# Layer 3's delta rule in half tiles, its query sums on TensorE, and two norms beside the collecting

## The chip, the cores and the metric

The kernel runs on one core of a Trainium2 chip, in one launch. A core has a matrix engine (PE, TensorE; its weight loads are listed apart as PEld), a vector engine (DVE), an activation engine (ACT, ScalarE), a general engine (POOL, GpSimd) and a queue engine (SP) that issues transfers. Each engine runs its own instructions in the order in which they were built into its stream, and waits on semaphores for the others. SBUF is the large on-chip memory. PSUM holds what PE writes; a tile of 128 x 512 fp32 fills one of its eight banks, and ACT and DVE can read and write it.

The metric is the device time of a launch in microseconds (us), the median over the runs. Before the change it is 4753.9 us, from three runs of 4752.63, 4753.9 and 4770.15. Lower is better.

## The reference

Four layers work on 4096 token columns of 128 features, held on the chip as `x`, 128 partitions by 4096 (8 tiles of 512). Each layer normalises and adds two branches:

```python
xn = _layernorm(x, axis=-1)          # (x - mean) / sqrt(var + 1e-5)
x = x + attention(xn, ...) + feed_forward(xn, ...)
```

Layers 0 and 2 end with experts: every token collects its two weighted rows from a result table in device memory and adds them to `x`. Layer 0 adds a shared dense branch besides.

Layer 3's attention is a delta rule. Queries and keys are convolved, passed through Silu and divided by their norms; per head (8 wide) a state `S` of 8 x 8 is carried over the tokens:

```python
def step(S, inp):
    q_t, k_t, v_t, b_t = inp
    v_new = (v_t - jnp.einsum('bhd,bhdm->bhm', k_t, S)) * b_t[..., None]
    S = S + jnp.einsum('bhd,bhm->bhdm', k_t, v_new)
    o_t = jnp.einsum('bhd,bhdm->bhm', q_t, S)
    return (S, o_t)
```

Layer 3's feed-forward is a pair of dense products with a sine between them:

```python
hidden = jnp.einsum('bsd,df->bsf', x, W1) + b1
imag = w_imag * jnp.sin(theta + hidden * 0.1)
quantum_phase = jnp.cos(theta) * w_real + jnp.sin(theta) * w_imag
act = jax.nn.relu(hidden + quantum_phase * imag * 0.1)
return jnp.einsum('bsf,fd->bsd', act, W2) + b2
```

## The kernel before

**Norm.** `_layer_norm` goes over the eight tiles. A matmul with a matrix of 1/128 (L292) gives the mean in PSUM, DVE subtracts it (L293), ACT squares (L295), four narrow matmuls (L297) give the variances of 512 tokens. When all tiles are through, one copy (L304), one Sqrt (L305) and one reciprocal (L306) follow for all 4096 tokens, and a second pass spreads the reciprocals over the features (POOL copy L273, PE transposes L276) and multiplies (L316).

**Collecting.** `_collect` fetches, for each group of 128 tokens and each of their two experts, 128 rows with one indirect transfer that POOL issues (L1031). DVE weights and adds them (L1039, L1041), PE transposes (L1042, into `cl_tp`, two PSUM banks), DVE adds to `x` (L1044). `_together` runs generators side by side, one tile of each in turn: in layer 0 the shared dense branch and the collecting, in layer 2 the collecting alone.

**Layer 3.** `_layer3` loads and prepares the weights, calls the norm, and then builds everything in a fixed order (`manual_schedule`: each engine's stream follows the order of the Python statements). Three convolutions of four taps per tile (L1743 matmuls, L1751 Silu) write to device memory, and the results are fetched back in another layout (heads on partitions, 32 chunks of 32 tokens along the row).

`_delta_rule` then works in three stages, on rows of 1024 (chunk, value, key) fp32 per partition, two PSUM banks for a state tile:

1. *States*, 32 steps: for all chunks but the last at once, two recurrences run. `sm` carries the map of a chunk's start state to its end, `sn` the state that grows from zero. Each step: `pro` = state times key (DVE, L1879), `dd` = its sum over the key (DVE, L1882), minus the value for `sn` (L1885), `u` = `dd` times key (DVE, L1890); PE rewrites the state as an identity times its copy minus an identity times `u` (`add`, L1871, four matmuls), and ACT copies the new state (`hist`, `dprod`, L1896). Within these steps the queries' squares are summed by DVE, eight pieces (L1916).
2. *Scan*, 31 steps: each chunk's start state from the one before it (L1944, L1951, L1952), on DVE, into an SBUF tile. Ahead of it stand a Sqrt of the query sums (L1804), a maximum, a reciprocal and a product (L1805, L1806, L1938).
3. *Outputs*, 32 steps over all 32 chunks from their true start states, with one state tile `sm` of 32 chunks. POOL multiplies the copied state by the query (L1985), after a small copy (`pace`, L1983) that makes it wait for `u`; DVE sums that product two steps later (L1961).

`_waves` is the feed-forward, a pipeline of 32 items (8 tiles by 4 quarters of the hidden width). Every call moves five items on by one stage each: `close` (L2050, DVE, every fourth item), `leave` (L2046, PE), `rest` (L2039 DVE, L2040 ACT relu), `fold` (L2033 and L2034 on DVE, L2035 Sin on ACT) and `enter` (L2025 PE, then L2027, L2029, L2030 on ACT). `_delta_rule` yields after every step of states and scan and once in an output step, and the loop in `_layer3` calls the waves at some of these yields:

```python
for n, _ in enumerate(_delta_rule(k, s, wl)):
    if n % 2 if n < 32 or n >= 63 else n % 6 == 2:
        next(waves, None)
```

So in states and outputs one item passes every second step, in the scan one every sixth.

Of the kernel before, what the change touches and what calls it, by code (L numbers as in the profile page):

```python
# [10 lines left out]
F32 = mybir.dt.float32  # L11
# [268 lines left out]
def _layer_norm(k, second=None):  # L280
# [4 lines left out]
    with tc.tile_pool(name="ln", bufs=3) as w, tc.tile_pool(  # L285
        name="ln_ps", bufs=5, space=PSUM
    ) as k.misc, tc.tile_pool(name="ln_st", bufs=1, space=PSUM) as sp:
        st = sp.tile([P, W], F32, name="ln_st")
        for t in range(NT):
            c = slice(t * W, (t + 1) * W)  # L290
            mean = k.misc.tile([P, W], F32, name="misc")
            nc.tensor.matmul(mean, k.mean, k.x[:, c], start=True, stop=True)  # L292
            nc.vector.tensor_tensor(k.xn[:, c], k.x[:, c], mean, ALU.subtract)  # L293
            sq = w.tile([P, W], F32, name="sq")
            nc.scalar.activation(sq, k.xn[:, c], AF.Square)  # L295
            for i in range(4):
                nc.tensor.matmul(  # L297
                    st[:, 4 * t + i : 4 * t + i + 1],
                    sq[:, i * P : (i + 1) * P],
                    k.mean[:, 0:1],  # L300
                    start=True,
                    stop=True,
                )
        nc.vector.tensor_copy(k.var, st[:, :TT])  # L304
# [714 lines left out]
def _collect(k, got, res, acc):  # L1019
# [3 lines left out]
    with tc.tile_pool(name="cl", bufs=6) as g, tc.tile_pool(name="cl_ps", bufs=2, space=PSUM) as ps:  # L1023
# [59 lines left out]
def _layer0(k, a):  # L1083
    _layer_norm(k)
    with k.tc.tile_pool(name="keep0", bufs=1) as keep:
# [7 lines left out]
        _together(_shared(k, a, k.x), _collect(k, got, k.res[0], k.x))  # L1093
# [417 lines left out]
def _layer1(k, a):  # L1511
    _layer_norm(k, (k.eps6, k.vec("l1_g"), k.vec("l1_b"), k.xl))
    _attention1(k, a)
    _local_layers(k, a)
# [171 lines left out]
def _layer2(k, a):  # L1686
    _layer_norm(k)
    with k.tc.tile_pool(name="keep2", bufs=1) as keep:
# [14 lines left out]
        _together(_collect(k, got, k.res[1], k.x))  # L1703
# [65 lines left out]
def _delta_rule(k, s, wl):  # L1769
# [97 lines left out]
    def add(st, w, u, first, last):  # L1867

        c = u.shape[1]
        for n in (slice(0, 16), slice(16, c)):  # L1870
            nc.tensor.matmul(st[:, n], w, u[:, n], start=first, stop=last)  # L1871

    def differ(st, now, i, c, values, parts=1):


        pro = room("pro")
        for n in range(parts):
            own = slice(n * c // parts, (n + 1) * c // parts)
            nc.vector.tensor_tensor(pro[:, own], st[:, own], _bc(kp[:, i, own], 2, 4), ALU.mult)  # L1879
        add(st, k.ident, now()[:, :c], True, False)  # L1880
        d = w.tile([P, CH, 4], F32, name="dd")
        nc.vector.tensor_reduce(d[:, :c], pro[:, :c], AX.X, ALU.add)  # L1882
        yield
        if values:
            nc.vector.tensor_tensor(d[:, :c], d[:, :c], vp[:, i, :c], ALU.subtract)  # L1885
        yield update(st, d, i, c)

    def update(st, d, i, c, first=False):
        u = room("u")
        nc.vector.tensor_tensor(u[:, :c], _bc(d[:, :c], 3, 8), _bc(kp[:, i, :c], 2, 4), ALU.mult)  # L1890
        add(st, k.neg_ident, u[:, :c], first, True)
        return u

    def copy(name, st, c):
        now = room(name)
        nc.scalar.copy(flat(now[:, :c]), flat(st[:, :c]))  # L1896
        return now
# [6 lines left out]
    ends = CH - 1  # L1904
    add(sm, k.ident, _bc(k.unit.rearrange("p (v d) -> p v d", d=8), 1, ends), True, True)
    mm, nn = copy("hist", sm, ends), None
    squares = ip.tile([P, 4, 8, P], F32, name="dvo")

    def query_norms(c):
        if 0 <= c < 8:  # L1910
            own = slice(c * P, (c + 1) * P)
            nc.scalar.activation(squares[:, c % 4], qraw[:, :, own], AF.Square)
        if 1 <= c < 9:
            own = slice((c - 1) * P, c * P)
            sq = squares[:, (c - 1) % 4]
            nc.vector.tensor_reduce(rq[:, own], sq.rearrange("p d t -> p t d"), AX.X, ALU.add)  # L1916
# [305 lines left out]
```

## Time and profile before

| | us |
|---|---|
| median of the runs | 4753.9 |
| the profiled execution, whole | 4760.1 |
| its span | 4758.3 |
| layer 0: shared branch with collecting | 1148 to 1311 |
| norm behind it, first half | 1311 to 1324.6 |
| layer 2: collecting | 3870 to 3969.6 |
| norm ahead of layer 3 | 3969.6 to 3995.9 |
| convolutions and fetching | 3995.9 to 4094 |
| states | 4094 to 4381 |
| before the scan | 4381 to 4395.6 |
| scan | 4395.6 to 4449.5 |
| outputs | 4449.5 to 4706.9 |
| output norm and product | 4706.9 to 4758.3 |

Times inside the profile are counted from the start of its span. A table of stages gives, for each stretch, the busy time of every engine with the number of its instructions, the TensorE clock that was granted (1.00 is full speed) and the share of time in which the transfer engines were at work. A line of a timeline gives start, duration, engine, line and operation, the tile written and the tiles read, shapes, and in brackets how long the engine had been idle and what it waited for.

### The profile page before, as it was taken

To read this page: it belongs to the slowest core of one execution; us is meant where nothing else is said; L and a number is where in the kernel's file an instruction comes from. 1 tells how busy PE (TensorE), PEld (TensorE's weight loads), DVE (VectorE), ACT (ScalarE), POOL (GpSimd) and SP (SyncE) were. 2 spreads that over 40 slices of the span, in tenths; PEclk is the share of its full clock that TensorE was granted. 3 is DMA by queue.
4 is the path that set the end of the run, shared out by engine and by line. 5 is a ranking of instruction groups with operands and counts; after the bars stand their busy time and mean duration, and the time that the engine had idled before them with its cause. 6 is when DMAs were issued, how large, how long until landed. Compare 5 with 4: busy or idle time off the path is not lost. (4 is left out here: it accounts for less than half of the span.)

```text
span 4758.3 us, 54361 instructions
## 1 busy us (share of the span) xinstructions
PE 3887.6 (82%) x20924; PEld 1774.2 (37%) x20924; DVE 3111.6 (65%) x4404; ACT 2562.6 (54%) x3611; POOL 649.7 (14%) x639
## 2 busy tenths in 40 slices
PE   4679999998968888888877888888879966888564
PEld 3223333364332222222224555555534543333221
DVE  5868989722336656565657888888465323899876
ACT  1257877831259999999984555455422112344331
POOL 1310000003100000000003232233103122000132
PEclk6689999999967777777778999999889987999788
DMA  2411121021221010100002111111100223300001
GB/s 86 118 41 55 29 59 26 11 72 49 14 83 58 18 49 18 36 27 18 18 13 65 36 41 35 40 34 32 37 0 23 63 64 83 97 0 9 0 0 53
DMA packets 107494, 191.81 MB, mean 40 GB/s; under 512 B 23138, under 2 KB 48354, under 8 KB 105378
## 3 DMA queue, kind: packets, MB, share of 16 engines
q1 hardware_dynamic: 98756, 166.31, 12.3%
q0 software_dynamic: 8192, 16.79, 1.7%
q10 hardware_dynamic: 288, 5.24, 0.3%
q8 instruction: 165, 2.70, 0.2%
q14 instruction: 93, 0.76, 0.1%
HBM read 95.00 MB, written 67.39 MB: 34 GB/s over the span
## 5 line engine op out<-in xcount | busy, mean ns | idle before, releaser
L740 DVE TENSOR_TENSOR p<-p,e 128x1024 f32<-128x1024 f32 x512 | 586.7, 1221 | 321.7 <-ACT e L738 321.7
L723 PE MATMUL big<-q,k 32*128 32x512 f32 x2048 | 560.3, 633 | 180.6 <-ACT p L734 74.9
L533 DVE TENSOR_REDUCE m<-mx 128x2 f32<-128x1024 f32 x512 | 620.9, 1223 | 101.4 <-PE mx L525 94.2
L418 PE MATMUL av<-p,v 128*32 128x256 f32 (+1 forms) x5632 | 666.4, 528 | 0.3
L616 ACT ACTIVATE p<-s 128x512 f32<-128x512 f32 x1024 | 550.9, 597 | 184.7 <-PE s L607 171.5
L723 PEld LDWEIGHTS big<-q,k 32*128 32x128 f32 x2048 | 210.8, 229 | 707.0 <-ACT e L738 347.3
L607 PE MATMUL s<-q,k 64*128 64x512 f32 x1024 | 277.7, 494 | 48.4 <-DMA q<-mrows 33.4
L738 ACT ACTIVATE e<-big,neg_mu 128x1024 f32<-128x1024 f32 x256 | 262.0, 1125 | 11.7 <-PE big L723 11.4
L525 PE MATMUL mx<-k,q 64*128 64x512 f32 x1024 | 238.8, 437 | 32.3 <-DVE m L533 17.8
L734 ACT ACTIVATE p<-big,neg_mu 128x1024 f32<-128x1024 f32 x256 | 261.2, 1199 | 3.0 <-PE big L723 2.8
L738 ACT ACTIVATE e<-big 128x1024 f32<-128x1024 f32 x256 | 243.0, 1040 | 28.8 <-PE big L723 27.2
L734 ACT ACTIVATE p<-big 128x1024 f32<-128x1024 f32 x256 | 239.4, 1076 | 8.2 <-PE big L723 8.1
L1177 POOL TENSOR_TENSOR lqk<-lt 128x512 f32<-128x512 f32 x128 | 162.5, 1269 | 518.1 <-DVE lt L1168 461.3
L1150 PE MATMUL lps<-f_wqkv,lh 128*128 128x512 f32 x384 | 215.2, 649 | 11.7 <-DVE lo L1305 6.8
L1871 PE MATMUL sm<-hist,in_const_sb 128*128 128x512 f32 x252 | 144.0, 701 | 93.1 <-ACT hist L1896 79.5
L1031 POOL DMA_INDIRECT cl_row<-res,back x128 | 121.2, 947 | 713.7 <-DMA in_l_su_sb<-in_l_su 474.3
L418 PEld LDWEIGHTS av<-p,v 128*32 128x32 f32 x5632 | 121.3, 111 | 253.1 <-issue 202.6
L607 PEld LDWEIGHTS s<-q,k 64*128 64x128 f32 x1024 | 107.5, 184 | 284.9 <-issue 162.3
L1268 ACT ACTIVATE lsm<-lsm 128x512 f32<-128x512 f32 x128 | 80.6, 630 | 222.1 <-DVE lsm L1267 220.7
L1896 ACT COPY hist<-sm 128x992 f32<-128x992 f32 (+1 forms) x65 | 64.9, 999 | 224.0 <-DVE pro L1879 143.4
L950 POOL DMA_INDIRECT buf<-xtok,to x128 | 125.9, 983 | 407.7 <-DMA buf<-xtok,to 221.3
L1143 POOL MEMSET lva<- 128x32 f32 x16 | 2.4, 152 | 1148.1 <-PE av L418 1148.1
(412 smaller groups left out, 6888.5 us busy)
## 6 DMA issues: line engine op xcount, KB each, us to landing
hl<-phi SPq DMA_DIRECT2D x64, 256.0 KB, 2.9
hl<-plo SPq DMA_DIRECT2D x64, 256.0 KB, 3.5
lvs<-lva SPq DMA_DIRECT2D x16, 520.0 KB, 5.7
q<-hl SPq DMA_DIRECT2D x32, 256.0 KB, 5.2
k<-hl SPq DMA_DIRECT2D x32, 256.0 KB, 5.9
q<-hl SPq DMA_DIRECT2D x16, 512.0 KB, 5.3
k<-hl SPq DMA_DIRECT2D x16, 512.0 KB, 3.5
lvs<-lva SPq DMA_DIRECT2D x16, 390.0 KB
```

What stands on the lines that cost most here:

```text
L418: k.nc.tensor.matmul(av[32 * j : 32 * j + 32, cols], v[:, kc, 9 * (4 * g + j) : 9 * (4 * g + j) + 32], pts[j][:, cols], start=kc == 0, sto ...
L525: nc.tensor.matmul(ps[:, i, :], q[rows, gg, qt * P : (qt + 1) * P], key[rows, gg, half * W : (half + 1) * W], start=True, stop=True, tile_ ...
L533: nc.vector.tensor_reduce(m[:, qt, gg, :, half], ps, AX.X, ALU.max)
L607: nc.tensor.matmul(ps, key[rows, half, kc * P : (kc + 1) * P], q[rows, half, qh * W : (qh + 1) * W], start=True, stop=True, tile_position= ...
L616: nc.scalar.activation(p, ps, AF.Exp, scale=8.0**-0.5)
L723: nc.tensor.matmul(ps[:, jj, :], key[rows, kc * P : (kc + 1) * P], q[rows, qh * W : (qh + 1) * W], start=True, stop=True, tile_position=(3 ...
L734: nc.scalar.activation(p, ps, f, bias=bias, scale=scale)
L738: nc.scalar.activation(e, ps, f, bias=bias, scale=scale)
L740: nc.vector.tensor_tensor(p, p, e, ALU.mult)
L1150: nc.tensor.matmul(ps, z.h[:, t * P : (t + 1) * P], wqkv[:, own], start=True, stop=True)
L1177: nc.gpsimd.tensor_tensor(z.qk[t][:, own], r[0], r[1], ALU.add)
L1871: nc.tensor.matmul(st[:, n], w, u[:, n], start=first, stop=last)
```

## The change

*Norms.* A generator `_norm_beside` runs beside the collecting. At layer 0 (`whole` is false) it takes means, differences, squares and variances of each tile as soon as `x` has it, with one PSUM bank for itself and one fewer for `cl_tp`; `_layer_norm` then begins at the Sqrt. At layer 2 it does the whole norm tile by tile, and `_layer3` has none.

*Weights.* Layer 3's loads and the preparation of its weights move into `_weights3`, ahead of layer 2.

*States.* `dd` lies in a PSUM bank of its own, in four turns. The query sums become eight matmuls with the identity that add up in a bank of the waves (`qh`), and an ACT copy. The waves' banks go from three to two. The Sqrt stands in step 18.

*Scan.* The start states are written straight into the PSUM state tiles.

*Outputs.* Chunks 0 to 15 and 16 to 31 are two PSUM tiles (`sm`, `sn`), each two banks, and each half runs through `differ` by itself: product, copy, adds, sum, difference, `u`. The `pace` copy is gone. There are two yields per step.

*Waves.* The argument is kept in turns instead of radians. A call now does half of the stages, either (`close`, `leave`, `sine`) or (`rest`, `enter`, `fold`), with `fold` a subtraction on POOL and the clamp on DVE in `sine`. The halves come at every second yield in states and outputs and at two of three in the scan.

```diff
+def _centre(k, t, misc, w):
+    nc = k.nc
+    c = slice(t * W, (t + 1) * W)
+    mean = misc.tile([P, W], F32, name="misc")
+    nc.tensor.matmul(mean, k.mean, k.x[:, c], start=True, stop=True)
+    nc.vector.tensor_tensor(k.xn[:, c], k.x[:, c], mean, ALU.subtract)
+    sq = w.tile([P, W], F32, name="sq")
+    nc.scalar.activation(sq, k.xn[:, c], AF.Square)
+    return sq
...
+def _norm_beside(k, whole):
+    nc, tc = k.nc, k.tc
+    with tc.tile_pool(name="nb", bufs=3) as w, tc.tile_pool(
+        name="nb_ps", bufs=2 if whole else 1, space=PSUM
+    ) as misc:
+        squares = {}
+        def variance(t):
+            st = misc.tile([P, W], F32, name="misc")
+            sq, own = squares.pop(t), slice(4 * t, 4 * t + 4)
+            for i in range(4):
+                nc.tensor.matmul(
+                    st[:, i : i + 1], sq[:, i * P : (i + 1) * P], k.mean[:, 0:1], start=True, stop=True
+                )
+            nc.vector.tensor_copy(k.var[:, own], st[:, :4])
+            if whole:
+                nc.scalar.activation(k.inv[:, own], k.var[:, own], AF.Sqrt, bias=k.eps5)
+                nc.vector.reciprocal(k.inv[:, own], k.inv[:, own])
+        def scale(t):
+            c = slice(t * W, (t + 1) * W)
+            spread = w.tile([P, 4, P], F32, name="nb_s")
+            nc.scalar.copy(spread, _bc(k.inv[:, 4 * t : 4 * t + 4], 2, P))
+            ps = misc.tile([P, W], F32, name="misc")
+            for i in range(4):
+                nc.tensor.transpose(ps[:, i * P : (i + 1) * P], spread[:, i], k.ident)
+            nc.vector.tensor_tensor(k.xn[:, c], k.xn[:, c], ps, ALU.mult)
+        for t in range(NT + 2):
+            if whole and t >= 2:
+                scale(t - 2)
+            if 1 <= t <= NT:
+                variance(t - 1)
+            if t < NT:
+                squares[t] = _centre(k, t, misc, w)
+            if t < NT:
+                yield
...
-        _together(_shared(k, a, k.x), _collect(k, got, k.res[0], k.x))
+        _together(_shared(k, a, k.x), _collect(k, got, k.res[0], k.x, 1), _norm_beside(k, False))
...
-    _layer_norm(k, (k.eps6, k.vec("l1_g"), k.vec("l1_b"), k.xl))
+    _layer_norm(k, (k.eps6, k.vec("l1_g"), k.vec("l1_b"), k.xl), True)
...
-        _together(_collect(k, got, k.res[1], k.x))
+        _together(_collect(k, got, k.res[1], k.x, 2), _norm_beside(k, True))
...
+    turns = itertools.cycle(range(4))
+    dd = s.d_ps.tile([P, 4, CH, 4], F32, name="dd")
+    turn = lambda: dd[:, next(turns)]
...
+    def differ(st, now, i, own, values):
         pro = room("pro")
-        for n in range(parts):
-            own = slice(n * c // parts, (n + 1) * c // parts)
-            nc.vector.tensor_tensor(pro[:, own], st[:, own], _bc(kp[:, i, own], 2, 4), ALU.mult)
-        add(st, k.ident, now()[:, :c], True, False)
-        d = w.tile([P, CH, 4], F32, name="dd")
-        nc.vector.tensor_reduce(d[:, :c], pro[:, :c], AX.X, ALU.add)
-        yield
+        nc.vector.tensor_tensor(pro[:, own], part(st, own), _bc(kp[:, i, own], 2, 4), ALU.mult)
+        add(st, k.ident, now(), own, True, False)
+        d = turn()
+        nc.vector.tensor_reduce(d[:, own], pro[:, own], AX.X, ALU.add)
         if values:
-            nc.vector.tensor_tensor(d[:, :c], d[:, :c], vp[:, i, :c], ALU.subtract)
-        yield update(st, d, i, c)
-    def update(st, d, i, c, first=False):
+            nc.vector.tensor_tensor(d[:, own], d[:, own], vp[:, i, own], ALU.subtract)
+        update(st, d, i, own)
...
-            sq = squares[:, (c - 1) % 4]
-            nc.vector.tensor_reduce(rq[:, own], sq.rearrange("p d t -> p t d"), AX.X, ALU.add)
+            sums = s.q_ps.tile([P, W], F32, name="qh")[:, :P]
+            for d in range(8):
+                nc.tensor.matmul(sums, k.ident, squares[:, (c - 1) % 4, d], start=d == 0, stop=d == 7)
+            nc.scalar.copy(rq[:, own], sums)
...
+        if i == 18:
+            nc.scalar.activation(rq, rq, AF.Sqrt)
...
-    inverse(rq)
-    nc.vector.tensor_scalar(rq, rq, 8.0**-0.5, None, ALU.mult)
-    start = ip.tile([P, L], F32, name="from_unit").rearrange("p (c v d) -> p c v d", v=4, d=8)
-    nc.vector.memset(start[:, 0], 0.0)
+            nc.sync.dma_start(both[m][HALF[other], ends], mm[HALF[m], ends])
+    nc.vector.tensor_scalar(rq, rq, 1e-6, 8.0**0.5, ALU.max, ALU.mult)
+    nc.vector.reciprocal(rq, rq)
+    st = [states(t) for t in ("sm", "sn")]
+    at = lambda c: st[c // 16][:, c % 16]
+    nc.vector.memset(at(0), 0.0)
...
-        nc.vector.tensor_tensor(start[:, c + 1], r, nn[:, c], ALU.add)
+        nc.vector.tensor_tensor(at(c + 1), r, nn[:, c], ALU.add)
...
+        hist = room("hist")
+        for half, own in enumerate(both_halves):
+            if i < N:
+                differ(st, lambda: copy(hist, st, own), i, own, True)
+            else:
+                copy(hist, st, own)
+            if half == 0 and i >= 2:
+                output(i - 2)
+            if half == 0:
+                yield
         if i:
-            if u is not None:
-                nc.gpsimd.tensor_copy(s.pace, u[:, 0, 0, 0:1])
             prod = room("dprod")
             nc.gpsimd.tensor_tensor(prod, hist, _bc(q_at[:, :, :, i - 1], 2, 4), ALU.mult)
+        yield
...
     def fold(z):
-        nc.vector.scalar_tensor_tensor(z.arg, z.turns, -TWO_PI, z.arg, ALU.mult, ALU.add)
-        nc.vector.tensor_scalar(z.arg, z.arg, PI_F32, -PI_F32, ALU.min, ALU.max)
-        nc.scalar.activation(z.arg, z.arg, AF.Sin)
+        nc.gpsimd.tensor_tensor(z.arg, z.arg, z.turns, ALU.subtract)
+    def sine(z):
+        nc.vector.tensor_scalar(z.arg, z.arg, 0.5, -0.5, ALU.min, ALU.max)
+        nc.scalar.activation(z.arg, z.arg, AF.Sin, scale=2.0 * PI_F32)
...
-    stages = (enter, fold, rest, leave, close)
-    for n in range(len(items) + 4):
-        for m in (4, 3, 2, 1, 0):
-            if 0 <= n - m < len(items):
-                stages[m](items[n - m])
-        yield
+    at = lambda n: items[n] if 0 <= n < len(items) else None
+    for n in range(len(items) + 3):
+        for parts in (((close, 3), (leave, 2), (sine, 1)), ((rest, 1), (enter, 0), (fold, 0))):
+            for fn, m in parts:
+                if at(n - m):
+                    fn(at(n - m))
+            yield
...
-            s.st_ps, s.q_ps, s.q_out = bank("st_ps", 1), bank("q_ps", 3), bank("qo_ps", 1)
+            s.st_ps, s.q_ps, s.q_out = bank("st_ps", 1), bank("q_ps", 2), bank("qo_ps", 1)
+            s.d_ps = bank("d_ps", 1)
...
-                if n % 2 if n < 32 or n >= 63 else n % 6 == 2:
+                if n % 3 if 32 <= n < 63 else n % 2:
```

## The prediction

> **What bounds the kernel now.** I read the engine table and the slices first, then the chain of waits, then a table of stages, then the timelines of the stages that the diff touches. No engine bounds the whole: PE is busy 82% of the span and DVE 65%. The chain that ended last passes mostly through the recurrence of layer 3:
>
> ```profile
> PE sm L1871 3%; DVE pro L1879 2%; DVE dd L1882 2%; DVE u L1890 2%; PE qh L1743 1%; ACT hist L1896 1%; POOL cl_row L1031 1%; DVE scan_r L1951 0%; DMA cl_row<-res,back 0%; DVE scan L1944 0%; DVE drq L1916 0%; DMA rows_b<-dprod 0%; DVE qhid L2039 0%; DVE qarg L2033 0%; PE qo L2046 0%
> ```
>
> The stages, with each engine's busy time and the granted clock:
>
> ```profile
> core 0: us, PE busy (x) PEld busy (x) DVE busy (x) ACT busy (x) POOL busy (x), PEclk, DMA share, GB/s
> 1148.00:1300.00 152.00, 152.00 (x351) 60.51 (x351) 56.95 (x120) 32.09 (x54) 38.07 (x40) 1.00 0.19 18
> ...
> 3870.00:3969.00 99.00, 26.64 (x96) 14.61 (x96) 27.79 (x76) 2.86 (x5) 60.42 (x64) 0.58 0.23 47
> 3969.00:4003.00 34.00, 29.95 (x129) 20.48 (x130) 14.20 (x26) 8.45 (x12) 4.79 (x8) 0.83 0.17 55
> ...
> 4094.00:4381.00 287.00, 257.95 (x569) 101.97 (x568) 273.81 (x299) 117.44 (x148) 0.00 (x0) 0.99 0.06 13
> 4381.00:4396.00 15.00, 3.57 (x8) 1.06 (x6) 8.66 (x7) 6.41 (x8) 0.00 (x0) 0.69 0.21 44
> 4396.00:4441.00 45.00, 14.75 (x19) 5.32 (x20) 42.31 (x121) 17.19 (x25) 0.00 (x0) 0.58 0.00 0
> 4441.00:4702.00 261.00, 176.06 (x309) 66.70 (x307) 191.15 (x250) 73.05 (x92) 92.15 (x62) 0.86 0.00 0
> ```
>
> So: the collecting of layer 0 (1148) is PE without a gap; that of layer 2 (3870) is POOL's 64 gathers with PE, DVE and ACT nearly idle; the states (4094) are DVE, with PE at 90% close behind; the scan (4396) is DVE; the outputs (4441) are full on no engine. There the chain goes round:
>
> ```profile
> 4562.91 1.29 DVE L1879 TENSOR_TENSOR pro<-sm,dk 128x512 f32<-128x512 f32 x2 [1.02 <-PE sm L1871]
> 4564.29 1.01 ACT L1896 COPY hist<-sm 128x1024 f32<-128x1024 f32 x1 [5.26 <-DVE pro L1879]
> 4565.35 1.98 PE L1871 MATMUL sm<-hist,in_const_sb 128*128 128x512 f32 x4 [2.55 <-ACT hist L1896]
> ...
> 4568.89 1.88 PE L1871 MATMUL sm<-u,neg_ident 128*128 128x512 f32 x4
> 4570.88 1.29 DVE L1879 TENSOR_TENSOR pro<-sm,dk 128x512 f32<-128x512 f32 x2 [1.12 <-PE sm L1871]
> ```
>
> `pro` reads the PSUM state, then ACT copies it, then PE adds the copy back and subtracts `u`, and only then can DVE begin again. DVE waits for that in 31 of the 33 steps, 64.7 us in all:
>
> ```profile
> DVE pro L1879 <- PE sm L1871: 64.7, 31, 3.8
> ```
>
> Last, the norm ahead of layer 3 stands alone between the final `x` of layer 2 and the first convolution:
>
> ```profile
> 3968.91 0.69 DVE L1044 TENSOR_TENSOR x<-x,cl_tp 128x512 f32<-128x512 f32 x1 [0.57 <-PE cl_tp L1042]
> ...
> 3986.90 0.19 DVE L304 COPY var<-ln_st 128x32 f32<-128x32 f32 x1 [2.17 <-PE ln_st L297]
> ...
> 3995.93 4.55 PE L1743 MATMUL qh<-xn,tap_w 128*128 128x512 f32 x10 [0.97 <-DVE xn L316]
> ```
>
> **The change, part by part.** The sum is made against the profiled execution: span 4758.3, 4760.1 us in all, 6.2 above the median of 4753.9.
>
> *Norm beside layer 0's collecting.* The first half of the next norm (mean, difference, square, variances) took 1311 to 1324.6 on its own, 13.5 us. It now runs in the stage where PE is full: per tile a mean (0.86) and four variances (0.5), 1.4 x 8 = 11 us added to PE. Of the 13.5 a tail of some 4 us stays for the last tile, so 9.5 go. The mean also stands behind `x += cl_tp` in PE's order: about five matmuls (4.3 us) cover a wait that measured 4.6 (1193.87 to 1198.46). One PSUM bank fewer for `cl_tp` makes that tighter. Bounds -4 and +8; I take +2.
>
> *Norm beside layer 2's collecting.* From 3969.6 to 3995.9 nothing but the norm runs: 26.3 us. Now each tile is normed while POOL, issuing gathers every 1.25 us, sets the pace; PE has 26.6 of 99 us in use and takes 8 x (0.9 mean, 0.5 variances, 0.8 spreading) = 18 more, DVE (27.8) takes some 15, ACT (2.9) some 15. If that cover were gone it would cost these 26 us again. What remains after the last `x` is one tile's chain: mean 0.9, difference 0.7, square 0.6, variances 0.95, copy 0.2, root 0.3 with perhaps its table load 1.28, reciprocal 0.35, spreading 0.6 + 0.8, product 0.7, with the gaps about 8 us. But PE does not stand idle in it: the build order puts five of the 24 groups of four convolution matmuls among the last collecting, 17 us of the 89 that PE needs, and more ready ones into the tail. So the convolutions end about 26 - 8 + 17 = 35 us sooner. Against it: DVE takes the gathered rows in order, and some now stand behind norm operations that wait for PE and ACT (Silu and Sqrt by turns reload tables, 1.28 each, four more of L311's kind); the row pool's six buffers are 7.5 us of gathers, so I charge little. Bounds -40 and -8; I take -34. The weights of layer 3, loaded and prepared before layer 2 (six products of 0.3 to 0.7 us), I cost at nothing: they lie beside layer 2's first norm, and without that cover they are 4 us of DVE.
>
> *States.* Before, 32 steps x 7.42 (4254.84 to 4262.26) = 237.4, 16 wave items x 1.72 = 27.5, eight query sums x 1.82 = 14.6, four closings 2.6 and 4.4 of small set-up make 286.5 of the 287. After: the steps stay 237.4, if reducing into PSUM and reading it back costs as much as SBUF. The row for that: `pro` from PSUM takes 1184 ns and `u` from SBUF alone 1192, same size, so I take nothing; the bounds are -2 and +6. Wave halves come every second step, so only eight items pass here, each 0.66 + 0.35 because the fold (0.68) goes to POOL: 8, with closings 1.3 and set-up 4.5. The sums go to PE: eight 128x128 matmuls of two passes, 16 x 0.12 (L1005's 34 in 4.06) = 1.9, with an ACT copy behind. In those eight steps PE needs 4 x 1.76 + 1.9 + 0.4 = 9.4 against DVE's 8, so PE becomes the bound and 11 come back. Sum 262: -25 (bounds -38, PE hidden, and -12).
>
> [...]
>
> *Before the scan.* Sqrt with its table (1.28 + 1.06) moves into step 18, and the last multiplication (0.69) is fused; the 6.55 reciprocal stays. From 14.6 to about 7.5: -7. The root's ACT time lies in ACT's idle share there (117 of 287 busy).
>
> *Scan.* Before: 31 x 1.40 + 6 items x 1.75 = 53.9 (4395.6 to 4449.5). Now wave halves come in two of three steps, some ten items instead of six, and they form a loop: `rest` 0.74, relu 0.72, argument 0.69, two roundings 0.72 each, POOL's fold 1.27 (L1177's row for 128x512), then the clamp on DVE, 0.43, and two scan steps 2.8 before the next `rest`. In the order the clamp stands only one scan step behind the `rest`, so DVE, and the scan steps queued behind the clamp, wait some 3 us per item. The loop is 8.1 us per three steps: 31/3 x 8.1 less a little at the ends = 81, +27. Bounds: no wait, 31 x 1.40 + 10 x 1.2 = 55, and with one more microsecond per item 91. This is the term that I am least sure of, and it goes against the change.
>
> *Outputs.* Before 4449.5 to 4706.9, 257.4 for 33 steps. Two halves in separate banks let ACT and PE work on one while DVE works on the other; the 64.7 us of waits go. DVE per step then: 1.29 + 1.22 + 0.29 + 1.23 + 1.21 = 5.24, 0.2 more for the splitting, and waves 0.74 + 0.43 + a quarter of 0.75 per two steps, 0.68: 6.1 x 33 = 202. What is late next: in a step where an item enters, the copy of the second half stands on ACT behind relu, argument and roundings (2.85), and on POOL the product (2.86) behind the fold (1.27). Counted from `rest`: roundings done at 3.7, fold 5.05, product 7.9; DVE reaches the reduction of that product at 5.2 and waits 2.7. Sixteen items: 42. Sum 244; I take 246, since part of the steps ran at the lower clock (0.86 granted on the mean): -11. Bounds 202 and 317, the latter below.
>
> The clock itself is open: in the scan `qh` matmuls took 1.91 us against 0.86 at full clock, and nothing in the trace says how the new mix of gaps is granted; PE's load of some 58% of the new step is close to that of before (176 of 261).
>
> **Sum.** +2 - 34 - 25 - 7 + 27 - 11 = -48: 4712 against 4760.1, and 4706 against the median.
>
> **Rivals.** (a) The norm's gain is lost: gathers are held by DVE's mixed order, or the pools let the norm begin only when the collecting ends. For: rows wait in order. Against: 6 buffers, idle engines. Three of four parts lost: +26, 4732.
> (b) No wave waits: scan 55, outputs 202, from an order in which clamp and product come late enough. Against: the fixed queues. 4706 - 26 - 42 = 4638; half of it, 4670.
> (c) Slower: PE stays at the low clock through the whole output stage and becomes its bound. A cold step is two times 3.8 (four matmuls, L1871 at 4581.27 took 3.63) and a wave matmul of 2.0: 9.6 x 33 = 317, +71 against my 246: 4777. It decides from a mean step of 8.9 us on (4754). For: the first output steps, straight from the cold scan, begin that way. Against: 0.86 granted before with longer waits.
>
> **Numbers.** Chances: mine 0.52, (a) 0.2, (b) 0.13, (c) 0.15. Mine alone 4685 to 4730. The range 4655 to 4772 leaves out the full (b) and the worst of (c). About 0.5% (24 us) is what a measurement can tell from no change: faster takes nearly all of mine and (b) and a third of (a), 0.69; the same, 0.19, is the rest of (a) and a part of (c); slower 0.12.
>
> **What would show it.** Right: first convolution within 5 us of the last `x`; a state stage near 262 with steps 11 to 18 longest; a scan of groups of three, one long; DVE's waits in the outputs on POOL's `dprod`, no longer on `sm`. Wrong: gathers further apart than 1.25 us, `clamp` never waiting for POOL, a granted clock near 0.6 in the outputs.

## The result and the profile after

The changed kernel takes 4740.9 us, the median of 11 runs (4735.9 to 4746.3); the kernel before took 4762.7 in the 11 runs beside them. The ratio is 0.9961 with a 95% interval of 0.9951 to 0.9972: faster by 0.39%, which is inside the 0.5% that I called no change. Forecast was a gain of 1.0%. The direction held; less than half of the size came.

The unchanged kernel's own median moved between 4743 and 4768 us from one session on the chip to another. So each experiment below is read by its ratio to the runs beside it, and by the lengths of stages in its profile.

The profiled execution of the changed kernel took 4742.0 us with a span of 4740.2, 18.1 below the 4758.3 of before. Stage by stage, from the two traces:

| stage | before, us | after, us | moved | forecast |
|---|---|---|---|---|
| layer 0's first gather to the end of the next norm | 232.9 | 232.9 | 0 | +2 |
| layer 2's first gather to its last `x` | 83.4 | 95.3 | +11.9 | |
| last `x` to the last convolution matmul | 124.9 | 108.5 | -16.4 | (both) -34 |
| states and the work before the scan | 301.1 | 270.1 | -31.0 | -32 |
| scan | 53.9 | 82.0 | +28.1 | +27 |
| outputs | 257.4 | 244.3 | -13.1 | -11 |

The rest, +2.4, is a later start out of layers that the change doesn't touch, and 0.2 at the end. The table of stages of the changed kernel, columns as in the one of before:

```profile
core 0: us, PE busy (x) PEld busy (x) DVE busy (x) ACT busy (x) POOL busy (x), PEclk, DMA share, GB/s
3889.00:3984.00 95.00, 43.25 (x134) 24.16 (x135) 31.86 (x95) 16.89 (x25) 61.17 (x64) 0.59 0.24 50
3984.00:4093.00 109.00, 92.92 (x221) 39.16 (x220) 54.49 (x36) 37.14 (x48) 0.00 (x0) 0.94 0.50 129
4093.00:4356.00 263.00, 249.98 (x665) 113.63 (x664) 242.82 (x261) 98.17 (x120) 8.88 (x7) 0.99 0.06 13
4356.00:4363.00 7.00, 3.54 (x8) 1.06 (x6) 6.95 (x4) 3.63 (x5) 1.26 (x1) 1.00 0.54 114
4363.00:4445.00 82.00, 35.99 (x38) 11.04 (x38) 51.50 (x148) 33.87 (x51) 12.65 (x10) 0.55 0.00 0
4445.00:4689.00 244.00, 179.54 (x314) 62.73 (x314) 196.58 (x321) 83.65 (x138) 108.63 (x46) 0.88 0.00 0
```

In the states PE is now busy for 250 of 263 us; in the scan DVE, full before, has 30 us of gaps; in the outputs DVE has 47. The chain of waits says what fills them: two POOL lines are new in it, the product `dprod` and the fold `qarg`, and PE's `sm`, which led the chain of before with 3%, has fallen to 0%:

```profile
PE gacc L1681 2%; PE qh L1793 1%; PE misc L1666 1%; POOL dprod L2041 1%; PE up L1046 1%; PE gp L1045 1%; POOL qarg L2091 1%; DVE dd L1944 1%; DVE pro L1941 1%; PE out_ps L1055 1%; PE big L1621 1%; PE sm L1927 0%; DVE u L1951 0%; DVE dvo L2025 0%
```

What DVE waited for (total us, times, longest), in the outputs and then in the scan:

```profile
DVE dvo L2025 <- POOL dprod L2041: 36.1, 15, 2.9
```

```profile
DVE qarg L2094 <- POOL qarg L2091: 28.0, 10, 3.0
```

The stage that went wrong is the collecting of layer 2. From its timeline (start, duration, engine, line; in brackets the idle time before and the releaser):

```profile
3916.68 1.06 PE L320 MATMUL misc<-in_const_sb,nb_s 128*128 128x128 f32 x4
...
3929.21 0.95 POOL L1081 DMA_INDIRECT cl_row<-res,back  x1 [0.30 <-issue]
...
3931.93 0.69 DVE L321 TENSOR_TENSOR xn<-xn,misc 128x512 f32<-128x512 f32 x1 [13.09 <-remote]
...
3933.15 0.95 POOL L1081 DMA_INDIRECT cl_row<-res,back  x1 [2.99 <-DVE xn L321]
```

The four transposes that spread the reciprocals end at 3917.7 in PE's records. DVE's product of them begins at 3931.9: PE's signal came only at 3931.91. Meanwhile DVE could weight no rows, the row buffers filled, and POOL paused. "Remote" is the profile's word where no recorded end fits the signal.

### The profile page after: what moved, and what is told of

The parts are those of the page before. It is cut to its first block, busy times and chain, and to the rows that moved or that the text cites. A ratio compares the mean times of both kernels' runs of the same rounds, so it can differ in the third digit from the quotient of the medians.

```text
span 4740.2 us, 54727 instructions
## 1 busy us (share of the span) xinstructions
PE 3911.8 (83%) x21048; PEld 1791.9 (38%) x21048; DVE 3093.1 (65%) x4481; ACT 2583.1 (54%) x3674; POOL 685.3 (14%) x632
## 5 line engine op out<-in xcount | busy, mean ns | idle before, releaser
L788 ACT ACTIVATE e<-big,neg_mu 128x1024 f32<-128x1024 f32 x256 | 262.2, 1126 | 12.5 <-PE big L773 12.3
L1049 DVE TENSOR_TENSOR h<-h,up 128x640 f32<-128x640 f32 x64 | 52.6, 821 | 159.9 <-PE up L1046 80.7
L575 PEld LDWEIGHTS mx<-k,q 64*128 64x128 f32 x1024 | 108.5, 195 | 62.9 <-DVE m L583 46.8
```

Of the source, the lines that this page charges most:

```text
L575: nc.tensor.matmul(ps[:, i, :], q[rows, gg, qt * P : (qt + 1) * P], key[rows, gg, half * W : (half + 1) * W], start=True, stop=True, tile_ ...
L788: nc.scalar.activation(e, ps, f, bias=bias, scale=scale)
```

## The experiments

The kernels ran in five sessions. e20 leaves out the clamp of the sine's argument; all others compute the whole reference. "Late signals" below are waits like the 13.09 us one above, for a PE whose records ended long before.

### The norm beside the collecting, taken apart

The first four ran in one session (before: 4742.9 us).

e1_norm_behind puts the norm of layer 3 back behind the collecting:

```diff
-        _together(_collect(k, got, k.res[1], k.x, 2), _norm_beside(k, True))
+        _together(_collect(k, got, k.res[1], k.x, 2))
...
+        _layer_norm(k)
```

> The changed kernel, with layer 3's norm in one piece behind the collecting of layer 2 again (its weights stay prepared ahead). In the changed kernel's profile the collecting is 95.3 us from the first gather to the last x (83.4 before), and the convolutions end 108.5 us after it (124.9 before). Theory A (the norm beside the collecting is worth almost nothing, because it holds the gathers up): 3 to 6 us slower than the changed kernel, with the collecting back at 83 to 84 us. Rival B (it is worth its forecast 34 us, and something else in the stage lost it, such as the earlier weights): some 25 us or more slower, or the collecting still 95.

4747.7 us, ratio 1.0009 (1.0000 to 1.0019). Collecting 83.6 us, and 134.0 behind it. The collecting is as short as theory A has it, but the kernel is 27 us slower than e2 beside it, not 3 to 6: the norm beside was worth something here.

e2_rows16 gives the collecting of layer 2 sixteen row buffers for six:

```diff
+def _collect(k, got, res, acc, banks, deep=6):
-    with tc.tile_pool(name="cl", bufs=6) as g, tc.tile_pool(name="cl_ps", bufs=banks, space=PSUM) as ps:
+    with tc.tile_pool(name="cl", bufs=deep) as g, tc.tile_pool(name="cl_ps", bufs=banks, space=PSUM) as ps:
...
-        _together(_collect(k, got, k.res[1], k.x, 2), _norm_beside(k, True))
+        _together(_collect(k, got, k.res[1], k.x, 2, 16), _norm_beside(k, True))
```

> The changed kernel, with sixteen row buffers instead of six in layer 2's collecting, so that POOL can issue far ahead of DVE. Theory A (POOL is held because rows wait in DVE's order for norm operations): gathers run through at 1.26 us, 81 us in all, the collecting falls from 95 to 84 to 87 us, and the whole by 8 to 11. Rival B (DVE and PE are late by themselves, and what is gained at POOL is given back in the tail): the collecting stays above 92 and the whole changes by less than 4.

4720.8 us, 0.9957 (0.9941 to 0.9974). Collecting 84.2, behind it 109.0.

e3_warm adds six matmuls per tile beside the collecting, in a bank of their own, whose results are not read; e7_convs_behind adds one. Both take one more PSUM bank, and in their profiles the convolutions start only when the collecting has ended:

```diff
+def _keep_warm(k, n):
+    nc, tc = k.nc, k.tc
+    with tc.tile_pool(name="kw_ps", bufs=1, space=PSUM) as ps:
+        idle = ps.tile([P, W], F32, name="kw")
+        for t in range(NT):
+            for _ in range(n):
+                nc.tensor.matmul(idle, k.ident, k.x[:, t * W : (t + 1) * W], start=True, stop=True)
+            yield
...
-        _together(_collect(k, got, k.res[1], k.x, 2), _norm_beside(k, True))
+        _together(_collect(k, got, k.res[1], k.x, 2), _norm_beside(k, True), _keep_warm(k, 6))
```

> The changed kernel, with six added matmuls per tile of 512 columns into a bank of their own beside the collecting of layer 2, whose results nobody reads, so that TensorE's granted clock should stay above the 0.5 of this stage; their bank also keeps the first convolutions behind the collecting. Theory C (what is late in this stage are PE's completions at the low clock: up to 16 us between the end that the profile gives a transpose or a variance and the semaphore that tells of it): clock 0.9 or more, no idle time of DVE above 3 us that waits for PE, collecting 83 to 87. Rival D (the gathers themselves hold PE's completions up, whatever the clock): the late completions stay, collecting 92 or more.

4737.2 us, 0.9987 (0.9977 to 0.9996): granted clock 0.81 in the gathers, collecting 90.4, behind it 116.7. Neither is what theory C expected (0.9 and 83 to 87).

> As the run with six added matmuls, with one per tile only: the convolutions stand behind the collecting just as there, and PE stays cold. It tells apart the clock from the place of the convolutions. Theory C: clock 0.5, late completions as in the changed kernel, collecting 92 to 97. Rival E (the early convolutions and their Silu, with the table loads on ACT, are what holds the norm up): late completions gone, collecting 83 to 87.

4723.0 us, 0.9961 (0.9947 to 0.9976): collecting 84.1, behind it 114.9.

Taken alone, e2 and e7 would have said that deeper buffers, or later convolutions, cure the collecting. But no profile of these four kernels, e1 and e3 among them, shows a single wait of an engine over 1.5 us on a signal that the trace can't place; the profile of the changed kernel has eight, 49 us in all, and that of before two, 18 us. Since e1, e2 and e7 are free of them at granted clocks of 0.55, 0.57 and 0.64 (3880 to 3930, where the changed kernel had 0.59), a low clock alone does not bring them. In e7 the collecting waits for gathers alone:

```profile
DVE cl_y L1099 <- DMA cl_row<-res,back: 33.8, 20, 11.6
DVE cl_y L1101 <- DMA cl_row<-res,back: 24.8, 22, 1.6
```

So the next question was whether one execution had misled me. e8_changed_again and e11_changed_third are the changed kernel once more, in two further sessions (before: 4763.6 and 4765.4).

> The changed kernel itself, beside the others of this call, for a second profile. It tells whether the late completions of PE in the collecting of layer 2 belong to the kernel or to one execution. Theory C (they belong to it): DVE again idles for 30 us or so in waits for PE that ended long before, collecting 92 to 98. Rival F (one execution's chance): collecting 84 to 86, and the whole about 10 us less relative to the kernel before than in the first profile.

4742.1 us, 0.9953 (0.9937 to 0.9970): collecting 95.3, behind it 108.5, and the same wait of 13.1 us at the same instruction.

> The changed kernel once more. The runs with no late completion of PE in layer 2's collecting (norm behind, sixteen rows, added matmuls) were on one chip, those with them (changed kernel, wave halves shifted, third bank) on another, and on the first chip the kernel before took 4743 us, on the second 4764. Theory H (the late completions go with the chip): collecting of 95 with DVE idle for 13.1 us at one place on a chip where the kernel before takes about 4763, and of 84 without it where the kernel before takes about 4743. Theory C (they go with the kernel): 95 wherever it runs.

4745.3 us, 0.9954 (0.9937 to 0.9971): 97.8 and 109.0. It is no chance of one execution. Beside e11 the sixteen buffers ran again:

> Sixteen row buffers again, beside the changed kernel on the same chip. Theory A (POOL is held for want of row buffers, and depth cures it): about 10 us less than the changed kernel. Theory H: on a chip with late completions DVE still idles for PE, gathers run on at 1.26 us, but the collecting stays at 90 or more; on a chip without them both kernels collect in 84 and stand within 3 us.

4756.8 us, 0.9984 (0.9971 to 0.9997): collecting 112.3, the worst of all. Its waits:

```profile
DVE var L309 <- issue: 22.9, 3, 21.3
...
DVE xn L321 <- remote: 15.1, 1, 15.1
...
DVE x L1094 <- remote: 9.4, 1, 9.4
DVE xn L287 <- remote: 8.6, 1, 8.6
```

What had looked like a cure was the session. The last of these ran in a fourth session (before: 4758.7): three row buffers, and the convolutions behind once more.

> The changed kernel with three row buffers instead of six in layer 2's collecting. On one chip sixteen gave 112 us of collecting and six 98. Theory D (a wait of DVE for PE lasts until POOL pauses for want of row buffers): waits half as long, collecting 86 to 92. Rival (three buffers pace POOL by DVE and cost more than they save): collecting over 98. On a chip without late completions: 84 to 90, from the pacing alone.

4744.3 us, 0.9971 (0.9958 to 0.9984): 98.3 and 108.5. The longest wait is 8.2 us instead of 13.1, but the collecting is above the 86 to 92 of theory D.

> The changed kernel with one added matmul per tile, whose bank keeps the convolutions behind the collecting; on the chip without late completions 84.1 and 114.9. Theory D (the gathers alone hold PE up): on a chip with late completions they stay, collecting 92 or more. Theory E (the early convolutions have a part in it): they go, collecting 84 to 88.

4747.7 us, 0.9982 (0.9973 to 0.9992): 100.7 and 112.1, with waits that e7 did not have:

```profile
DVE xn L321 <- remote: 19.9, 2, 16.3
...
DVE x L1104 <- remote: 12.0, 2, 9.1
```

Neither the number of buffers nor early convolutions bring the late signals: they are there with three, six and sixteen buffers, and in e19 without early convolutions. Three buffers are about as good as six: 98.3 us, and 96.8 in e17 below, against 94.9 to 101.3 in the other profiles with late signals.

### The third bank

The convolutions and the betas work in `q_ps`, whose banks the change cut from three to two. I had overlooked that. PE's waits from 3960 to 4105 of the changed kernel, and of before from 3969 to 4105:

```profile
PE qh L1793 <- ACT hist L1801: 8.3, 3, 4.6
...
PE qh L1793 <- DVE dprod L1815: 5.0, 1, 5.0
```

```profile
PE qh L1743 <- ACT hist L1751: 6.4, 3, 4.6
```

e10_third_bank lets every third of these tiles use the bank of `dd`, which is free until the states:

```diff
+            def conv_bank():
+                if next(convs) % 3 < 2:
+                    return s.q_ps.tile([P, W], F32, name="qh")
+                return s.d_ps.tile([P, 4, 32, 4], F32, name="dd").rearrange("p t c v -> p (t c v)")
...
-        ps = s.q_ps.tile([P, W], F32, name="qh")
+        ps = s.conv_bank()
```

> The changed kernel, with the convolutions and the beta products of layer 3 in three banks by turns again (the bank of dd is free until the states begin). Theory G (two banks instead of three hold the convolutions: PE waits 13 us for Silu and for the copies of beta, 6 before, and only two groups can be begun beside the collecting): from the last x to the end of the convolutions 98 to 101 instead of 108.5, the whole -7 to -10. Rival (the stage is bound by transfers, whose share rises to 0.57 here): within 3 us of the changed kernel.

4731.8 us, 0.9927 (0.9911 to 0.9944), beside e8: collecting 95.5, behind it 98.0 for 108.5. The bank is worth 10.5 us. Of the two waits the longer one is left, and it is shorter:

```profile
PE qh L1793 <- ACT hist L1801: 6.6, 2, 4.6
```

e18_bank_behind adds to this e1's edit, in the fourth session:

> The changed kernel with the third bank for the convolutions and layer 3's norm behind the collecting: what the changed kernel would be without this part and without its cost to the convolutions. From the last x to the end of the convolutions 125 as in the kernel before (134 with two banks), collecting 83 to 84. Beside the run with the third bank and the norm beside (95 + 98) the norm beside would be worth 15 us on a chip with late completions, 26 on one without. Rival (the convolutions were held by something other than the banks): 130 or more.

4745.2 us, 0.9973 (0.9963 to 0.9984): 83.6 and 126.0, where before took 83.4 and 124.9 and e1, with two banks, 83.6 and 134.0. Its collecting waits for gathers only:

```profile
DVE cl_y L1091 <- DMA cl_row<-res,back: 39.6, 32, 1.6
DVE cl_y L1089 <- DMA cl_row<-res,back: 24.7, 27, 11.6
```

This is the session in which e16 and e19 show the late signals. e18's profile marks none as "remote", not even in layer 0, whose code is the same; but layer 0 takes 208.1 us from its first gather to its last `x` in e18 and 209.0 in e16, against 199.5 to 201.7 in the first session. And DVE idles there at the product that waits in e16 and in before, this time with no signal recorded at all:

```profile
1137.08 0.69 DVE L1116 TENSOR_TENSOR sh<-sh,sup 128x512 f32<-128x512 f32 x1 [6.71 <-issue]
```

So I read e18 as disturbed too, with a collecting that stays at 83.6 because the norm's PE work is not in it; one profile suggests that and doesn't prove it. With three banks the norm beside saves 209.6 - 193.5 = 16 us even with the late signals (e18 against e10); without them, with two banks, 217.6 - 193.2 = 24 (e1 against e2).

### The waits of the waves

e4_scan_phase moves the halves of the waves by one scan step, so that the clamp follows two steps behind the fold; e5_out_phase moves them by half an output step:

```diff
-                if n % 3 if 32 <= n < 63 else n % 2:
+                if n % 2 if n < 32 else n % 3 != 2 if n < 63 else n % 2:
```

```diff
-                if n % 3 if 32 <= n < 63 else n % 2:
+                if n % 2 if n < 32 else n % 3 if n < 63 else n % 2 == 0:
```

> The changed kernel, with the wave halves of the scan at other steps: two scan steps between an item's rest and the clamp of the next, one between clamp and rest, instead of the reverse. Theory (the clamp waits for the chain of relu, argument, roundings and fold, 4.1 us, behind one scan step of 1.4): the wait shrinks by a scan step, groups of three steps take 6.7 instead of 8.06, the scan 69 to 71 instead of 82, the whole -11 to -14. Rival (DVE's own work or the clock sets the groups): under 4 us.

4726.4 us, 0.9916 (0.9900 to 0.9933), beside e8. Scan 65.9 for 82.0, in groups of 1.40, 3.29 and 1.93, and the wait is less than half. That is below the expected 69 to 71, partly because one half fewer falls into the scan (20 for 21):

```profile
DVE qarg L2094 <- POOL qarg L2091: 12.9, 9, 1.6
```

> The changed kernel, with the wave halves of the output steps at the step's end instead of its middle, so that the copy of the second half stands on ACT ahead of relu, argument and roundings, and the product on POOL ahead of the fold. Theory (the 2.2 us of every second step are DVE's wait for POOL's product behind that chain): steps of 6.4 throughout, outputs 210 to 225 instead of 244, the whole -20 to -34. Rival (the wait only moves: the first half's copy stands behind the same chain in the next step, and PE's adds and the next product are late instead): outputs above 235.

4729.7 us, 0.9924 (0.9908 to 0.9941). Outputs 232.3 for 244: the gain came, but above the range. The wait for the product has gone, as it should:

```profile
DVE dvo L2025 <- POOL dprod L2041: 2.9, 2, 1.7
```

Yet DVE is busy for 222 of 232 us where it should need some 195. The timeline shows where: the clamp, 0.42 us everywhere in the changed kernel, now lasts to the end of POOL's product beside it.

```profile
4576.63 2.86 POOL L2041 TENSOR_TENSOR dprod<-hist,raw 128x1024 f32<-128x1024 f32 x1
4577.40 2.38 DVE L2094 TENSOR_SCALAR qarg<-qarg 128x512 f32<-128x512 f32 x1
```

The product ends at 4579.49, the clamp at 4579.78. All 14 clamps of the output stage took 1.72 to 3.06 us, 2.37 in the middle: 32 us in all, 26 more than at 0.42. A wait had turned into a longer instruction. e14_three joins e10, e4 and e5; e17_three_rows3 adds three row buffers; e15_quarters is e14 with `rest`, `enter` and `fold` each at a yield of its own in the outputs:

```diff
-        for parts in (((close, 3), (leave, 2), (sine, 1)), ((rest, 1), (enter, 0), (fold, 0))):
+        for parts in (((close, 3), (leave, 2), (sine, 1)), ((rest, 1),), ((enter, 0),), ((fold, 0),)):
...
+            part = itertools.cycle((1, 3))
...
+                if n > 63 or n < 63 and (n % 3 != 2 if n >= 32 else n % 2):
+                    for _ in range(1 if n >= 63 else next(part)):
+                        next(waves, None)
```

> Three edits together: the third bank for the convolutions, the wave halves at the other steps of the scan, and at the end of the output steps. Alone they gave -10.5, -16 and -12 by their stages. Theory (they lie in different stages and add up): 36 to 40 us less than the changed kernel, scan 66, outputs 231 to 233, from the last x to the end of the convolutions 98. Rival (the shifts share the waves: fewer halves in the scan leave items behind the last output step): 10 us of it lost at the end.

4712.3 us, 0.9891 (0.9874 to 0.9909): 33 us below e11 beside it, where 36 to 40 were expected. By the stages the three gains add up (behind the collecting 98.6 for 109.0, scan 66.0 for 82, outputs 232 for 244); the collecting, 101.3 for 97.8, gives 3.5 back.

> As the three edits together, but in the output steps the waves come in quarters, one at each of the two yields of a step: close, leave and sine; rest; enter; fold. So ACT never has more than 2.1 us of wave work between two copies of a state. Theory (what is left of the long output steps, 8.06 against 6.42, is ACT's 2.9 us of wave work ahead of a copy): steps of 6.4 to 7.0, outputs 210 to 222. Rival (the steps are bound elsewhere, by PE's order or POOL's product): outputs within 5 of the 232 of the halves.

4719.7 us, 0.9906 (0.9886 to 0.9927), outputs 244.0, 12 us more than with the halves, so neither the theory nor its rival held. Its clamps in the outputs took 3.03 us in the middle, held in the same way.

> Third bank, shifted wave halves in scan and outputs, and three row buffers. Stages as before alone: scan 66, outputs 232, convolutions 98 behind the last x, collecting as in the run with three row buffers. If theory D holds, 45 to 50 us less than the changed kernel (ratio to the kernel before 0.985 to 0.988); if not, no better than without the three buffers (0.989).

4709.1 us, 0.9899 (0.9882 to 0.9915): as e14, and not the 0.985 to 0.988 of theory D.

The last two, in a fifth session (before: 4768.3), test the held clamp on the kernel of e14. e20_no_clamp leaves it out; e21_clamp_two does the same clamp with an operation of two sources:

```diff
-        nc.vector.tensor_scalar(z.arg, z.arg, 0.5, -0.5, ALU.min, ALU.max)
```

```diff
+    floor = wp.tile([P, 1], F32, name="q_low")
+    nc.gpsimd.memset(floor, -0.5)
+    low = floor.to_broadcast([P, W])
...
-        nc.vector.tensor_scalar(z.arg, z.arg, 0.5, -0.5, ALU.min, ALU.max)
+        nc.vector.scalar_tensor_tensor(z.arg, z.arg, 0.5, low, ALU.min, ALU.max)
```

> The kernel of e14_three (third bank, scan and output shifted) with the clamp of the folded argument left out; the argument lies within half a turn by the rounding ahead of it. In e5_out_phase the 14 clamps of the output stage took 1.72 to 3.06 us, 2.37 in the middle, where those of the changed kernel take 0.42; each ended within 0.3 us of the end of POOL's product dprod that ran beside it. Theory I (the clamp is held until POOL's product ends, and that is why the outputs came to 232.3 and not 210 to 225): without it the outputs are 232.1 - 14 x 2.37 = 199, and with PE's 162 of 220 us and the loop through ACT close behind, 199 to 212. Rival K (the loop of copies, adds and states sets the step, and the clamp only fills a wait): outputs above 225. Scan: DVE no longer waits for POOL. By the loop theory of my prediction 31 x 1.40 + 10 items x 0.74 = 51 to 58; if the next rest then waits for the chain relu, argument, two roundings, fold and sine (0.72 + 0.69 + 1.44 + 1.27 + 0.63, with rest 0.74 some 5.5 against 4.2 + 0.74 of DVE's work in three steps) 57 to 63. Whole: 4712.3 - 20 to - 45.

4682.6 us, 0.9820 (0.9804 to 0.9837). The scan is 58.4, in the range of the longer chain: DVE's `rest` now waits for the sine on ACT, nine times, 7.5 us. The outputs are 221.3, between the two theories: DVE's busy time falls from 222 to 193, so the clamp did hold DVE; but two thirds of this go into a new wait, for PE:

```profile
DVE pro L1941 <- PE sm L1927: 19.3, 12, 2.3
DVE dvo L2025 <- POOL dprod L2041: 2.9, 2, 1.9
```

> The kernel of e14_three with the same clamp at the same place on DVE, as one SCALAR_TENSOR_TENSOR (minimum with 0.5, maximum with a broadcast column of -0.5) in place of the TENSOR_SCALAR: 0.7 to 0.75 us for 512 columns by rest's row, against 0.42. Theory I in the narrow form (only the quick form, 0.42 for 512 columns, is held by POOL's product): 14 x (2.37 - 0.74) = 23 us off the outputs, 205 to 214. Rival L (any DVE operation whose sources both lie in SBUF is held beside POOL's product): clamps of about 2.4 again and outputs 228 to 236. [...] Scan 66 to 69, by 0.3 more per item.

4709.4 us, 0.9874 (0.9858 to 0.9891), outputs 235.7, scan 68.6. The narrow form of my theory falls, the rival holds:

```profile
4540.58 2.86 POOL L2041 TENSOR_TENSOR dprod<-hist,raw 128x1024 f32<-128x1024 f32 x1
4542.00 1.99 DVE L2097 SCALAR_TENSOR_TENSOR qarg<-qarg,q_low 128x512 f32<-128x512 f32 x1
```

Free of POOL this form takes 0.69; beside the product 2.63 in the middle of the stage's fifteen. So it isn't only the form of 0.42 us that is held. `pro` and `u`, with one source in PSUM, keep their 0.68 and 0.69 us beside the same products; the clamp reads and writes SBUF alone in both its forms. What in the product holds the clamp, these runs don't show.

## Why the prediction was right and wrong

**Norm beside layer 0's collecting**, +2: 0 measured, and there is luck in it. Both profiles have late signals in this stage, 18.0 us of waits before and 15.2 after. In the session without them, e1, e2, e3 and e7 spent 8 to 13 us more than the kernel before ahead of layer 2's first gather. This is worked out: e2, for one, takes 22.1 us less in all, but 31.8 less from that gather on (840.3 against 872.1 in the only profile of before). So without late signals this part, or the weights that moved ahead of layer 2, seems to cost some 10 us; no profile of the kernel before from that session shows it directly.

**Norm beside layer 2's collecting**, -34 with bounds of -40 and -8: -4.5. This is the step that failed, and with it the sum, since all the others together are off by 2 us. Three things are in it:

1. The collecting grew by 11.9 us. I had charged "little" for DVE's order and the row buffers. The place was right, since DVE takes rows in order and POOL paused behind it by 3 to 4 us three times; the cause was not among those I priced. DVE waited up to 13 us, and 16 in e19, for results of PE whose records had long ended; in e2 and e7, without such waits, the collecting took 84.2 and 84.1. My own mark for a failure, gathers further apart than 1.25 us, is what the profile shows.
2. The convolutions lost a bank: 10.5 us by e10, 8 by e18 against e1. The diff says that the waves' banks go from three to two; my sum has no term for it, since I had not asked who else takes tiles from that pool.
3. I counted five groups of convolution matmuls, 17 us, ahead of the last `x`. In the order that was built some ten matmuls stand there, about 9 us at the 0.86 us of one at full clock, in e10 with its third bank as in the changed kernel.

Together 12 + 10 + 8 = 30 against the 29.5 that are missing. What is left for the norm's tail is 108.5 - 98.6 - 10 + 9 = 9 us, where 98.6 is the convolution stage of before (3995.9 to 4094.5); I gave it 8. The trace gives a little less: the norm's last product ends 12.3 us after the last `x`, and PE spends 6.3 of these on convolutions, which leaves 6. Why PE's signals are late stays open (see the last section).

**States and before the scan**, -25 and -7: -31.0 together. Steps 11 to 18 are the long ones, 8.44 and 9.30 us by turns against 7.44 and 8.09, and PE has no gap in them (8.44 us busy of 8.44, 9.30 of 9.30), as its bound there asked. Moving `dd` into PSUM cost next to nothing: `u` reading it took 1192 ns from PSUM and 1192 before from SBUF, the sum into PSUM 1195 against 1186. The +6 us that my bounds allowed for this is shown by no run.

```profile
L1951 DVE TENSOR_TENSOR u<-dd,dk 128x992 f32<-128x992 f32 x64 | 76.3, 1192 | 2.2
L1944 DVE TENSOR_REDUCE dd<-pro 128x124 f32<-128x992 f32 x63 | 75.3, 1195 | 2.2
```

**Scan**, +27: +28.1. The loop of 8.1 us per three steps is 1.93 + 4.70 + 1.40 = 8.03, and the clamp waits 3.0 us for POOL. e4 and e20 show that this wait is the term.

```profile
4396.16 0.43 DVE L2094 TENSOR_SCALAR qarg<-qarg 128x512 f32<-128x512 f32 x1 [2.99 <-POOL qarg L2091]
...
4404.19 0.43 DVE L2094 TENSOR_SCALAR qarg<-qarg 128x512 f32<-128x512 f32 x1 [2.99 <-POOL qarg L2091]
```

**Outputs**, -11: -13.1. DVE waits for the product in the steps where an item enters, 2.4 us each where I had 2.7, and the steps are 6.42 and 8.58.

```profile
4512.99 1.27 POOL L2091 TENSOR_TENSOR qarg<-qarg,qtmp 128x512 f32<-128x512 f32 x1 [5.18 <-ACT qtmp L2088]
...
4514.21 2.85 POOL L2041 TENSOR_TENSOR dprod<-hist,raw 128x1024 f32<-128x1024 f32 x1
4517.10 1.22 DVE L2025 TENSOR_REDUCE dvo<-dprod 128x128 f32<-128x1024 f32 x1 [2.39 <-POOL dprod L2041]
```

My lower bound of 202 without that wait left out the held clamp and the loop through PE: e5 reached 232, and even e20, with no clamp, 221, with 19.3 us of waits for PE.

**Rivals.** (a) had the right stage, its price of +26 against +29.5, and half of the cause: gathers were held behind DVE. (b) is excluded, waves wait in both stages. (c) is excluded by a granted clock of 0.88 in the outputs.

## What to carry to other kernels

When a pool loses a bank, list every stage that takes tiles from it, not only the one that the edit is about. When a wait between DVE and POOL is moved away, look at the durations too: in e5 the clamp of 0.42 us took 2.37 beside POOL's product, and no table of waits shows that. And before believing that an edit cured a stall, run the unedited kernel in the same session.

## What the runs showed that I had not expected

PE's results reached DVE much later than PE's records end: DVE waited 13.1 us at the same product in nine profiles from four sessions, 15.1 in e12, 16.3 in e19, and once, in e12, 21.3 with no signal recorded. The kernel before has it too, beside layer 0's gathers:

```profile
1140.54 0.69 DVE L1066 TENSOR_TENSOR sh<-sh,sup 128x512 f32<-128x512 f32 x1 [8.43 <-remote]
```

All the long ones lie where POOL issues gathers back to back (1.26 us apart in the changed kernel) and PE works beside them; without the norm's PE work the collecting keeps its 83.6 us in e18. It is present in every session but one, in which no profiled kernel has it, layer 0's collecting with the norm beside it is 6 to 11 us shorter (199.5 to 201.7 us against 208.1 to 210.9), and the kernel before takes 4743 us and not 4759 to 4768. What makes a session differ stays open: two sessions whose chips bear the same number fell on either side. Whether PE itself runs late there or only its signal, the trace can't tell. The changed kernel as it stands never ran in that session, so its worth there is known only by its neighbours e2 and e7, 0.9957 and 0.9961. These are the ratios of the other sessions too (0.9953 to 0.9961), since the kernel before also gains some 20 us where the signals are not late.

The best version is e20, 1.8% below the kernel before; of those that keep the clamp, e14, e17 and e21 lie together at 4709 to 4712 us, 1.0 to 1.3% below in their sessions.
